# Cross-attention block in f32: the first context rows in two halves around the scale weights, block 0 projected in seven half-size products, and the way in in another order

## The chip, the cores and the metric

The kernel runs on one core of one Trainium2 chip. The metric is the device time of one execution in microseconds (us); the text names a version's time by the median of its runs. The profile is of one execution.

## The reference

An adaptive layer norm in front of a cross attention with 16 heads, and a residual. All arrays are f32: x is (16, 1024, 512), the context (16, 64, 512), the condition (16, 512), the weights 512 x 512 or 512 x 1024.

```python
def _ada_ln(x, c, W_ss, b_ss):
    h = (x - mean(x)) / sqrt(var(x) + 1e-5)
    scale, bias = split(silu(c) @ W_ss + b_ss, 2)
    return (1.0 + scale)[:, None, :] * h + bias[:, None, :]

xq  = _ada_ln(x,   cond, Wss_q,  bss_q)
xkv = _ada_ln(ctx, cond, Wss_kv, bss_kv)
q = (xq @ Wq + bq).reshape(B, 1024, 16, 32)
k, v = split((xkv @ Wkv + bkv).reshape(B, 64, 2, 16, 32), axis=2)
attn = softmax(einsum(q, k) / sqrt(32))
out = einsum(attn, v).reshape(B, 1024, 512)
return x + (out @ Wp + bp)
```

## The kernel before

The 16 x 1024 query rows are cut into 32 *blocks* of 512 rows (two to a batch entry). The 16 x 64 context rows make two *groups*, A (batch entries 0 to 7) and B (8 to 15), of 512 rows each, so that a group's rows, features, keys and values have the shapes of a block.

Every 512 x 512 x 512 multiplication, but for some projections, is done in seven *products* of half-size blocks instead of eight (Strassen's scheme in Winograd's form): each is four matmuls of 128x256 (eight records in the trace). It needs sums and differences of half weights (`column_sums`, `weight_sums`, each in four steps) and of half features (`feature_sums`, `row_sums`), which GpSimd makes, and for group A's features VectorE. The products accumulate in two PSUM banks; partial results are evicted (`context_out`, `query_out`, `query_added`, `added`) and for some the first bank is copied into the second as a seed (`query_seed`). The seven are called here product 1 to 7 of keys, values, queries (of a block) or of the projection.

A block passes these steps. `load_x` brings its rows (pool `xpool` with two slots for all rows: A, 0, B, 1, 2, ... take them in turn, and a load waits until the last reader of the block two before is done). `q_stats` takes mean and variance of each of four row tiles on VectorE; `q_scale` makes the reciprocal deviation (ScalarE Ln and Exp, then four small operations, on GpSimd, for A on VectorE); `hidden` normalises on ScalarE. `turn` transposes within 32x32 squares on VectorE, and `move` sends the squares to their places in 16 DMAs (half of them, for block 1, from GpSimd's queue). `scale_features` applies scale and shift on ScalarE. Block 0 and the groups are instead transposed on TensorE (`turned_products`, `turned_features`) and scaled on their way out of PSUM (`turned_scaled`, `modulated`). Then come the seven query products; `score_products` twice, for two halves of the keys, into two PSUM tiles each, which `maximum` (VectorE) and `copied` (ScalarE) read one after the other; `maxima` spreads the row maxima; `subtract` (GpSimd), `weights` (Exp, ScalarE), `total` (GpSimd), `row_total`, `inverse_rows` (VectorE, then small DMAs through DRAM), `mix` (TensorE, weights times values), `spread_rows` and `divided` (VectorE), and the projection: `row_sums`, `biased`, seven times `product` and `added`, which also adds the residual and stores.

Block 0 is projected otherwise: `project_seed` writes the bias into a bank and `project_seeded` runs four matmuls of 128x512 into it, for each of its four row tiles, followed by `projected`.

The values of a group are evicted into a stage and sent by `value_move` in 16 DMAs to their places.

Nothing is reordered by a scheduler: under `tc.manual_schedule()` each engine, and SP's DMA queue, executes its instructions in the order in which the program emits them, and waits where data, buffers or PSUM tiles are not free. The emission order of the way in, from the first load to the start of the loop over blocks 3 to 29, is a list written out by hand at the end of the function, interleaving all of the above. From block 3 on a loop emits a fixed order; TensorE's first step there is the score products of block 3 (160.10 us in the profile).

At the start SP issues the condition, the four row tiles of group A, the first half of the context's scale and shift weights (`wss_kv`), a quarter of the key and value weights, and so on; TensorE runs 36 warm-up transposes and then `scale_shift_rows`, which turns the condition and these weights into scale and shift rows.

Of the kernel before, what the change touches and what calls it, by code (L numbers as in the profile page):

```python
# [15 lines left out]
P = 128  # L16
# [4 lines left out]
def cross_attention_block(  # L21
# [84 lines left out]
    def load_x(i):  # L106

        t = xpool.tile([P, NT, H], F32, tag="x", name=f"x_{i}")
        if i in GROUPS:
            b = GROUPS[i] * PER  # L110
            rows = context[b : b + PER].rearrange("b k h -> (b k) h")
            src = rows.rearrange("(t p) h -> p t h", p=P)
        else:
            src = rows_of(x, i)
        if i == "A":
            for k in range(NT):
                nc.sync.dma_start(t[:, k, :], src[:, k, :])
        else:
            nc.sync.dma_start(t, src)
        x_tiles[i] = t  # L120

# [175 lines left out]
    def rstd_of(mv, n, apart):  # L297

        rstd = small.tile([P, 2, n], F32, tag="rstdq", name="rstdq")
        work = small.tile([P, 4, n], F32, tag="workq", name="workq")  # L300
# [29 lines left out]
    def q_scale(i):  # L330
        apart = i != "A"
        q_rstd[i] = rstd_of(q_mv.pop(i), NT, apart)
# [6 lines left out]
    def hidden(i, ts):  # L339

        for t in ts:
            row, rstd = x_tiles[i][:, t, :], q_rstd[i]
            if i == "A" and t % 2 == 0:
                nc.vector.tensor_scalar(
                    row, row, rstd[:, 0, t : t + 1], rstd[:, 1, t : t + 1], ALU.mult, ALU.add
                )
            else:
                normalise(row, row, rstd, t)
# [43 lines left out]
    def turned_features(i, t):  # L392
# [10 lines left out]
        if t == NT - 1:  # L403
            x_tiles.pop(i)
# [151 lines left out]
    def query_product(i, n):  # L556
        seven(i, "q", n, (0, 1))
# [306 lines left out]
    def project_seed(i, t):  # L864
        pp_tiles[i, t] = bank(f"pp_{i}_{t}", 2 + t % 2)
        nc.scalar.copy(pp_tiles[i, t], b_p_sb)

    def project_seeded(i, t):
        pp = pp_tiles[i, t]
        for c in range(NC):  # L870
            nc.tensor.matmul(  # L871
                pp,
                lhsT=ot_tiles[i][:, c, t * P : (t + 1) * P],
                rhs=w_p_sb[:, c, :],
                start=False,
                stop=(c == NC - 1),
                skip_group_check=True,
            )

# [13 lines left out]
    def weight_sums():  # L893

        tt = nc.gpsimd.tensor_tensor
        WT = wt[0] = wpool.tile([P, 4, HC, HO], F32, tag="WT", name="WT")
        tt(WT[:, 0], half_weights(0, 1), half_weights(1, 1), ALU.add)
        tt(WT[:, 1], WT[:, 0], half_weights(0, 0), ALU.subtract)
        tt(WT[:, 2], half_weights(0, 0), half_weights(0, 1), ALU.subtract)
        tt(WT[:, 3], half_weights(1, 0), WT[:, 1], ALU.subtract)  # L900

# [100 lines left out]
    turned_features("A", 0)  # L1002
    hidden("A", (1,))
    column_sums("k", w_k_sb, w_k_sums, (2,))
    column_sums("v", w_v_sb, wv_sums, (0,))
    scale_shift_taken("kv", 0)
    scale_shift("kv", 2 * NC, 0)
    hidden("A", (3,))
    turned_features("A", 1)
    column_sums("v", w_v_sb, wv_sums, (2,))  # L1010
    modulated("A", 0, 0, nc.scalar)
    modulated("A", 0, 0, nc.vector)
    turned_features("A", 2)
    turned_features("A", 3)
# [8 lines left out]
    modulated("A", 1, 0, nc.scalar)  # L1023
    modulated("A", 1, 1, nc.scalar)
    modulated("A", 1, 1, nc.vector)
    context_out("A", "k", 1)
    context_product("A", "k", 2)
    feature_sums("A", nc.vector, (0,))
    context_product("A", "v", 2)
    context_out("A", "k", 2)  # L1030
    context_product("A", "k", 7)
    column_sums("v", w_v_sb, wv_sums, (1,))
    context_out("A", "v", 1)
    column_sums("k", w_k_sb, w_k_sums, (1,))
    context_out("A", "v", 2)
    feature_sums("A", nc.vector, (1,))
    feature_sums("A", nc.vector, (2,))
    load_x("B")
    context_product("A", "v", 7)
    context_out("A", "k", 7)  # L1040
    q_stats(0, (0,))
    q_stats(0, (1,))
    context_out("A", "v", 7)
    q_stats(0, (2,))
    feature_sums("A", nc.vector, (3,))
    context_product("A", "v", 6)
    scale_shift_rows("q", 0)
    context_product("A", "k", 6)
    q_stats(0, (3,))
    load_query_weights()  # L1050
    scale_shift_rows("q", 1)
    context_out("A", "v", 6)
    context_product("A", "v", 4)
    scale_shift_taken("q", 0, 2)
    load_projection_bias()
    q_scale(0)
    scale_shift("q", 0, 0, 2)
    q_stats("B", (0,))
    context_product("A", "v", 5)
    q_stats("B", (3,))  # L1060
    column_sums("v", w_v_sb, wv_sums, (3,))
    q_stats("B", (2,))
    hidden(0, (0,))
    hidden(0, (1,))
# [548 lines left out]
```

## Time and profile before

| what | value |
|---|---|
| time, 3 runs | median 1029.23 us (1028.48 to 1030.68) |
| the profiled execution | 1029.09 us, span from the first to the last instruction 1027.3 us |
| mean granted TensorE clock | 0.998 |
| busy: TensorE (PE) | 1008.1 us, 98% |
| busy: VectorE (DVE), GpSimd (POOL), ScalarE (ACT) | 860.8, 805.9, 639.7 us |
| DMA | 149.82 MB, mean 146 GB/s |

How to read the rows: a row of the timeline has start and duration in us, engine, line of the kernel, operation, output <- inputs, the shape, how many instructions are merged, and in brackets the engine's idle time before it with what released it. A row of the waits has who waited for whom, and the total, the number and the longest of these waits. A row of the chain of waits has start, duration and what the chain was made of at that time. A row of the windows has the stretch, its length, the busy time of PE, PEld (weight loads), DVE, ACT and POOL, then the granted clock, the DMA share and GB/s. A row of the groups has line, engine, operation, shapes, count, busy time, the mean in ns, and the idle time before.

### The profile page before, as it was taken

How to read it: one execution, taken by the hardware profiler on the slowest of the kernel's cores; microseconds unless marked ns; L12 is line 12 of the kernel's file. 1: busy time of each engine (PE TensorE's matmuls, PEld its weight loads, DVE VectorE, ACT ScalarE, POOL GpSimd, SP SyncE). 2: the span in 40 equal slices, each digit the busy share in tenths (PEclk: the TensorE clock that was granted, in tenths of full speed). 3: DMA queues.
4: the chain of work that ended last, by engine and by line, in shares of the span. 5: the costliest groups of instructions: out<-in, count | busy, mean ns of one | idle time of the engine just before them, and what ended most of it. 6: DMA issues, size and time to landing. Idle time of an engine off the chain costs nothing.

```text
span 1027.3 us, 21213 instructions
## 1 busy us (share of the span) xinstructions
PE 1008.1 (98%) x8077; PEld 763.3 (74%) x8077; DVE 860.8 (84%) x1174; ACT 639.7 (62%) x1025; POOL 805.9 (78%) x518
## 2 busy tenths in 40 slices
PE   7989999999999999999999999999999999999998
PEld 6768657777777777877777778777777777777756
DVE  6757988888988888889888888888888888876795
ACT  3577667666766666666666667666675666665530
POOL 4547798789888888898888888988888888987861
PEclk9999999999999999999999999999999999999999
DMA  9555645444554444445544544545534444335122
GB/s 314 174 133 142 179 134 145 156 158 154 161 166 130 127 148 138 145 154 163 165 126 131 163 124 152 155 156 165 162 100 149 131 159 152 115 123 166 45 85 85
DMA packets 112197, 149.82 MB, mean 146 GB/s; under 512 B 34104, under 2 KB 45392, under 8 KB 112096
## 3 DMA queue, kind: packets, MB, share of 16 engines
q1 hardware_dynamic: 111712, 147.94, 46.8%
q8 instruction: 64, 1.05, 0.5%
q0 software_dynamic: 384, 0.54, 0.3%
q14 instruction: 37, 0.30, 0.1%
HBM read 79.21 MB, written 34.60 MB: 111 GB/s over the span
## 4 chain that ended last, share of the span: by engine, by line
PE 88%; DMA 3%; DVE 3%; ACT 2%; SPq 1%; issue 1%; POOL 1%; DVEq 0%; ACTq 0%; POOLq 0%
PE pq L539 36%; PE pp L955 34%; PE ps L658 6%; PE po L826 6%; PE pp L871 1%; PE pv_B L539 1%; DMA x<-in_x_dram 1%; PE pv_A L539 1%; DMA xt<-ht 1%; PE pk_A L539 1%; DMA wss_kv<-in_L_xcond_Wss_kv_dram 1%; SPq L387 1%; DVE m L675 1%; ACT s L723 1%; ACT xk_B L421 0%
## 5 line engine op out<-in xcount | busy, mean ns | idle before, releaser
L717 POOL TENSOR_TENSOR s<-s,mb 128x2048 f32<-128x2048 f32 x64 | 290.3, 4561 | 125.7 <-DVE mb L704 125.7
L684 ACT COPY s<-ps 128x1024 f32<-128x1024 f32 x128 | 129.6, 1013 | 105.3 <-DVE m L675 63.7
L675 DVE TRANSPOSE_TENSOR_REDUCE m<-ps 128x32 f32<-128x1024 f32 x128 | 151.0, 1215 | 32.1 <-PE ps L658 32.1
L955 PE MATMUL pp<-w_p_sb,ot 128*128 128x256 f32 x720 | 165.5, 379 | 0.5 <-DVE r L979 0.4
L979 DVE TENSOR_TENSOR r<-pp,r 128x512 f32<-128x512 f32 x203 | 132.0, 671 | 33.6 <-PE pp L955 29.4
L578 ACT ACTIVATE qt<-pq,bias_t 128x256 f32<-128x256 f32 x256 | 106.0, 465 | 80.4 <-PE pq L539 80.1
L955 PEld LDWEIGHTS pp<-w_p_sb,ot 128*128 128x128 f32 x720 | 136.6, 190 | 20.3 <-issue 1.3
L723 ACT ACTIVATE s<-s 128x2048 f32<-128x2048 f32 x64 | 122.4, 1913 | 43.2 <-POOL s L717 43.1
L757 POOL TENSOR_TENSOR sum<-s,s 128x2048 f32<-128x2048 f32 x31 | 140.7, 4538 | 7.8 <-ACT s L723 7.8
L955 PEld LDWEIGHTS pp<-WT,s 128*128 128x128 f32 x480 | 86.5, 189 | 57.0 <-issue 31.0
L539 PE MATMUL pq<-xt,w_q_sb 128*128 128x256 f32 x512 | 122.5, 382 | 4.5 <-ACT xt L447 4.5
L539 PE MATMUL pq<-xt_sums,w_q_sums 128*128 128x256 f32 x512 | 123.0, 385 | 0.0
L539 PEld LDWEIGHTS pq<-xt_sums,w_q_sums 128*128 128x128 f32 x512 | 95.0, 190 | 35.2 <-issue 23.4
L539 PE MATMUL pq<-xt,w_q_sums 128*128 128x256 f32 x512 | 120.9, 379 | 0.0
L955 PE MATMUL pp<-WT,s 128*128 128x256 f32 x480 | 119.3, 391 | 0.2 <-POOL s L934 0.2
L955 PE MATMUL pp<-WT,ot 128*128 128x256 f32 x480 | 113.7, 380 | 0.6 <-POOL ot L931 0.6
L539 PEld LDWEIGHTS pq<-xt,w_q_sb 128*128 128x128 f32 x512 | 97.3, 191 | 21.3 <-ACT xt L447 5.7
L539 PEld LDWEIGHTS pq<-xt,w_q_sums 128*128 128x128 f32 x512 | 97.3, 190 | 13.6 <-DVE ht L365 0.2
L955 PEld LDWEIGHTS pp<-WT,ot 128*128 128x128 f32 x480 | 91.0, 190 | 14.4 <-issue 1.1
L447 ACT ACTIVATE xt<-xt,ss_q 128x512 f32<-128x512 f32 x124 | 94.4, 810 | 10.1 <-DMA V_A<-stage_A 5.3
L335 ACT ACTIVATE x<-x,rstdq 128x512 f32<-128x512 f32 x128 | 97.8, 810 | 2.1 <-POOL rstdq L312 2.1
L498 POOL TENSOR_TENSOR xt_sums<-xt 128x512 f32<-128x512 f32 x64 | 81.5, 1273 | 17.0 <-ACT xt L447 9.5
(176 smaller groups left out, 1506.3 us busy)
## 6 DMA issues: line engine op xcount, KB each, us to landing
x<-in_x_dram SPq DMA_DIRECT2D x32, 1024.0 KB, 6.2
r<-in_x_dram SPq DMA_DIRECT2D x32, 1024.0 KB, 5.4
xt<-ht SPq DMA_DIRECT2D x488, 64.0 KB, 2.0
out_dram<-r SPq DMA_DIRECT2D x58, 512.0 KB, 3.7
out_dram<-r SPq DMA_DIRECT2D x11, 256.0 KB, 2.2
wss_kv<-in_L_xcond_Wss_kv_dram SPq DMA_DIRECT2D x4, 512.0 KB, 8.6
wss_q<-in_L_xcond_Wss_q_dram SPq DMA_DIRECT2D x4, 512.0 KB, 11.0
vr<-ltd SPq DMA_DIRECT2D x128, 8.0 KB, 1.7
```

The lines of the kernel that those rows point to most:

```text
L335: nc.scalar.activation(dst, src, AF.Identity, bias=rstd[:, 1, j : j + 1], scale=rstd[:, 0, j : j + 1])
L447: nc.scalar.activation(xt[:, :, c, :], xt[:, :, c, :], AF.Identity, scale=ss["q"][:, c, b : b + 1], bias=ss["q"][:, NC + c, b : b + 1],)
L498: eng.tensor_tensor(dst, a, b, ALU.subtract)
L539: nc.tensor.matmul(out_, lhsT=lhsT, rhs=rhs, start=new and m == 0 and c == 0, stop=c == HC - 1, skip_group_check=True,)
L578: nc.scalar.activation(dst, src, AF.Identity, bias=bq_t[:, o : o + 1])
L675: nc.vector.tensor_reduce(m_tiles[i][:, z, 2 * e : 2 * e + 2, :], s_banks[i, z][e].rearrange("p r (j a) -> p r j a", a=32), AX.X, ALU.max, ...
L684: nc.scalar.copy(s_tiles[i, z][:, 2 * e : 2 * e + 2, :], s_banks[i, z][e])
L717: eng.tensor_tensor(s_tiles[i, z], s_tiles[i, z], mb_tiles[i], ALU.subtract)
L723: nc.scalar.activation(p, p, AF.Exp, scale=SCALE)
L757: nc.gpsimd.tensor_tensor(t, s_tiles[i, 0], s_tiles[i, 1], ALU.add)
L955: nc.tensor.matmul(acc[k][:, t * HO : (t + 1) * HO], lhsT=rows[:, c, t * P : (t + 1) * P], rhs=cols[:, c, :], start=n == 2 and t == 0 and ...
L979: nc.vector.tensor_add(r, a, r)
```

## The change

Three things change.

1. The four row tiles of group A are loaded in two pairs: tiles 0 and 1 ahead of the first scale weights, tiles 2 and 3 behind these and the first key weights. Their statistics, Ln, Exp and the four small VectorE operations are done for each pair apart (`first_scale(h)` in place of `q_scale("A")`).
2. Block 0 is projected like the others: `biased`, `row_sums`, seven `product`, `added`. `project_seed` and `project_seeded` are gone. `weight_sums` takes a step's number, so that its four sums can be emitted apart.
3. The list of the way in is emitted in another order, up to the loop. On SP's queue the projection bias goes from behind the query weights to behind the load of block 3, half of group A's value moves go ahead of that load, and the move of block 3 goes ahead of the transfer of block 0's row totals. The loop and the end are as before.

The helpers:

```diff
-        if i == "A":
-            for k in range(NT):
-                nc.sync.dma_start(t[:, k, :], src[:, k, :])
-        else:
-            nc.sync.dma_start(t, src)
+        nc.sync.dma_start(t, context_rows(i) if i in GROUPS else rows_of(x, i))
         x_tiles[i] = t
...
+    def load_first(k):
+
+        if k == 0:
+            x_tiles["A"] = xpool.tile([P, NT, H], F32, tag="x", name="x_A")
+        nc.sync.dma_start(x_tiles["A"][:, k, :], context_rows("A")[:, k, :])
...
-    load_x("A")
+    load_first(0)
+    load_first(1)
     load_scale_shift("kv", w_ss_kv, 0)
     load_context_weights(0, 0)
+    load_first(2)
+    load_first(3)
     load_scale_shift("kv", w_ss_kv, 1)
...
     def q_scale(i):
-        apart = i != "A"
-        q_rstd[i] = rstd_of(q_mv.pop(i), NT, apart)
+        q_rstd[i] = rstd_of(q_mv.pop(i), NT, True)
+
+    def first_scale(h):
+        q_rstd["A", h] = rstd_of(q_mv["A"][:, 2 * h : 2 * h + 2, :], 2, False)
...
-    def weight_sums():
+    def weight_sums(k):
```

The order, at the places that the prediction speaks of (each list is whole between its first and last line; "..." where lines are left out):

```diff
 start of group A: the old order (-), the new (+)
-    q_stats("A", (0,))
-    q_stats("A", (1,))
-    q_stats("A", (2,))
-    q_stats("A", (3,))
-    column_sums("k", w_k_sb, w_k_sums, (0,))
-    biases()
-    q_scale("A")
-    hidden("A", (0,))
-    hidden("A", (2,))
-    scale_shift_rows("kv", 0)
...
-    context_product("A", "k", 1)
-    scale_shift_rows("kv", 1)
-    modulated("A", 0, 1, nc.vector)
-    scale_shift_taken("kv", 1)
-    scale_shift("kv", 2 * NC, 1)
-    modulated("A", 0, 1, nc.scalar)
-    modulated("A", 1, 0, nc.vector)
-    context_product("A", "v", 1)
+    column_sums("k", w_k_sb, w_k_sums, (2,))
+    q_stats("A", (0,))
+    q_stats("A", (1,))
+    scale_shift_rows("kv", 0)
+    first_scale(0)
+    hidden("A", (0,))
+    biases()
+    scale_shift_taken("kv", 0)
+    scale_shift("kv", 2 * NC, 0)
+    turned_features("A", 0)
...
+    modulated("A", 0, 0, nc.scalar)
+    modulated("A", 0, 0, nc.vector)
+    q_stats("A", (3,))
+    load_x("B")
+    q_stats("A", (2,))
+    first_scale(1)
+    hidden("A", (2,))
+    hidden("A", (3,))
+    context_product("A", "k", 1)
+    scale_shift_rows("kv", 1)
+    scale_shift_taken("kv", 1)
+    turned_features("A", 2)
+    context_out("A", "k", 1)
+    column_sums("v", w_v_sb, wv_sums, (0,))
+    scale_shift("kv", 2 * NC, 1)
...
+    modulated("A", 1, 1, nc.scalar)
+    context_product("A", "k", 2)
+    context_product("A", "v", 1)
```

```diff
 after, around block 1's rows: statistics, normalising, turning, moving
+    q_stats(1, (3,))
+    context_product("A", "v", 4)
+    turned_features("B", 1)
+    value_move("A", 0)
+    column_sums("q", w_q_sb, w_q_sums, (1,))
+    q_stats(1, (1,))
...
+    turned_features("B", 0)
+    modulated("B", 0, 0, nc.vector)
+    turned_features("B", 3)
+    load_x(3)
+    turned_features("B", 2)
...
+    query_seed(0)
+    modulated("B", 1, 0, nc.scalar)
+    hidden(1, (0,))
+    query_product(0, 6)
+    query_product(0, 2)
+    context_out("B", "k", 1)
+    hidden(1, (1,))
+    turn(1, (0,))
...
+    turn(1, (3,))
+    query_out(0, 2)
...
+    move(1, two=True)
```

```diff
 after, score products of block 1 and the row total of block 0
+    score_products(1, 0)
+    context_out("B", "v", 6)
+    maximum(1, 0, 1)
+    row_total(0)
+    maximum(1, 0, 0)
+    context_product("B", "v", 5)
...
+    query_product(2, 1)
+    copied(1, 0, 1)
+    copied(1, 0, 0)
...
+    score_products(1, 1)
```

```diff
 before, block 0's projection (for t = 0 to 3, interleaved)
-    project_seed(0, t)
-    project_seeded(0, t)
-    projected(0, t)
...
-    weight_sums()
 after
+    row_sums(0, 0)
...
+    product(0, 2)
...
+    product(0, 1)
...
+    weight_sums(0)
+    weight_sums(2)
+    weight_sums(1)
...
+    row_sums(0, 1)
...
+    product(0, 7)
```

More of the change, by code (lines that the diff above doesn't have):

```diff
@@ L1077, in cross_attention_block @@
     q_scale("B")
[L1078 removed]
+    turned_scaled(3)
+    column_sums("q", w_q_sb, w_q_sums, (2,))
+    turned_scaled(1)
+    turned_scaled(0)
+    hidden("B", (0,))
+    load_x(2)
     q_stats(1, (0,))
[L1080 to L1081 removed]
+    hidden("B", (3,))
+    hidden("B", (1,))
+    feature_sums(0, nc.gpsimd, (0,))
+    q_stats(1, (2,))
     context_product("A", "k", 3)
[L1083 to L1084 removed]
@@ L1197, in cross_attention_block @@
-    feature_sums(1, nc.gpsimd, (2,))
-    query_out(1, 2)
-    maximum(0, 1, 0)
-    maximum(0, 1, 1)
-    maxima(0)
+    hidden(3, (0,))
+    maximum(0, 1, 1)
+    query_product(1, 2)
+    context_product("B", "k", 3)
+    maximum(0, 1, 0)
+    query_out(1, 2)
+    feature_sums(1, nc.gpsimd, (2,))
+    query_product(1, 7)
+    context_out("B", "k", 3)
+    feature_sums(1, nc.gpsimd, (3,))
+    maxima(0)
+    hidden(3, (3,))
+    q_stats(4, (0,))
+    copied(0, 1, 1)
+    move(2)
+    load_projection()
@@ L1366, in cross_attention_block @@
-    weights(2, 0)
-    subtract(2, zs=(1,))
-    row_sums(1, 0)
+    load_x(6)
+    biased(0, 3)
+    copied(2, 0, 0)
+    feature_sums(3, nc.gpsimd, (1,))
+    product(0, 7)
+    maximum(2, 0, 1)
+    maximum(2, 0, 0)
+    copied(2, 0, 1)
+    move(4)
+    added(0, 7)
+    query_out(3, 2)
+    score_products(2, 1)
+    product(0, 6)
+    maximum(2, 1, 0)
+    copied(2, 1, 0)
+    feature_sums(3, nc.gpsimd, (2,))
+    product(0, 4)
+    hidden(5, (2,))
+    maximum(2, 1, 1)
+    weight_sums(3)
@@ new lines, in cross_attention_block @@
+    added(0, 6)
+    product(0, 5)
+    feature_sums(3, nc.gpsimd, (3,))
+    q_stats(6, (0,))
+    copied(2, 1, 1)
+    maxima(2)
+    hidden(5, (3,))
+    inverse_rows(1)
+    hidden(5, (1,))
+    mix(1)
+    query_product(3, 7)
+    hidden(5, (0,))
+    subtract(2, zs=(0,))
+    turn(5, (0,))
+    q_stats(6, (2,))
+    turn(5, (1,))
+    added(0, 5)
+    added(0, 4)
+    product(0, 3)
+    query_out(3, 7)
+    scale_features(4, (2,))
+    subtract(2, zs=(1,))
+    query_product(3, 6)
+    spread_rows(1)
```

550 lines of the change are left out of this document (227 added, 323 removed).

## The prediction

> **What bounds the kernel now.** I read the page first, then for whom TensorE waited, then the chain of waits and the windows around the longest wait.
>
> ```profile
> span 1027.3 us, 21213 instructions
> ...
> PE 1008.1 (98%) x8077; PEld 763.3 (74%) x8077; DVE 860.8 (84%) x1174; ACT 639.7 (62%) x1025; POOL 805.9 (78%) x518
> ```
>
> TensorE's waits in the first 260 us (in total, times, longest):
>
> ```profile
> PE pq L539 <- ACT xt L447: 4.5, 1, 4.5
> PE pc L218 <- DMA early<-in_cond_dram: 2.6, 1, 2.6
> PE pq L539 <- ACT qt L578: 1.4, 1, 1.4
> PE pxk_B L400 <- DVE xk_B L419: 1.3, 1, 1.3
> PE pxk_A L400 <- DVE xk_A L419: 1.1, 1, 1.1
> PE ps_kv L256 <- DMA wss_kv<-in_L_xcond_Wss_kv_dram: 1.0, 1, 1.0
> PE po L826 <- ACT s L684: 0.4, 1, 0.4
> ```
>
> TensorE is busy for all but 19 us, and 12 of these lie here, nearly all in the way in. The loop from block 3 on is full, and the change leaves its order alone. So the question is when TensorE comes to the loop, at 160.1 us now, and with what behind it. From the chain of waits (start, duration, eight matmul records to a product):
>
> ```profile
> 76.79 3.03 PE pq L539 x8
> 79.83 2.37 PE pk_B L539 x8
> ```
>
> ```profile
> 122.28 3.43 PE pp L871 x8
> 125.71 1.73 PE pq L539 x8
> ```
>
> and from the windows (TensorE's granted clock is the third number from the end):
>
> ```profile
> 40.00:60.00 20.00, 18.66 (x95) 16.38 (x94) 13.51 (x37) 17.39 (x45) 15.35 (x20) 1.00 0.29 103
> ```
>
> ```profile
> 78.00:80.00 2.00, 2.00 (x6) 1.60 (x5) 1.97 (x4) 1.94 (x6) 1.27 (x1) 0.50 0.43 105
> ```
>
> A product takes 1.73 us. The two behind the 4.5 us wait took 3.03 and 2.37, 1.9 more than usual, at a clock of 0.50. I count 1.75 of it, so the longest wait costs 6.2 us in all. After the 1.3 us wait, which falls in 40 to 60 us, the clock stayed at 1.00.
>
> **The change, part by part.** I take the new order of each engine's instructions, give each the duration it has in these rows, and follow who waits for whom.
>
> *Block 0.* Four projections of 3.43 us, 13.72 in all, become seven products of 1.73, 12.11: 1.6 us less for TensorE. The price is four row sums on GpSimd, taken up below; the four weight sums are there before and after.
>
> *The first context rows.* From TensorE's timeline, twice, with the chain between:
>
> ```profile
> 8.88 0.41 PE L256 MATMUL ps_kv<-wss_kv,early 128*32 128x128 f32 x4
> 10.30 1.07 PE L256 MATMUL ps_kv<-wss_kv,early 128*32 128x128 f32 x28 [1.00 <-DMA wss_kv<-in_L_xcond_Wss_kv_dram]
> ```
>
> ```profile
> 14.70 1.73 PE pk_A L539 x8
> ```
>
> ```profile
> 38.47 5.44 DMA x<-in_x_dram
> 43.94 0.70 DVE bs L294
> 44.67 0.18 DVE mvq L295
> 44.85 0.57 DVE K_A L605
> 45.42 0.60 DVE stage_A L619
> 46.02 1.02 DVE xk_B L419 x4
> ```
>
> ```profile
> 48.45 1.89 PE L539 MATMUL pq<-xt,w_q_sb 128*128 128x256 f32 x8
> ```
>
> Two of the four row pieces now go behind the scale weights. At most 1.4 us is to be had (8.88 to 10.30); I take 1.25, so the scale rows start at 9.05. The bias transpose and its two vector copies now lie behind them (about 0.5), while eight transposes (about 1.1) are no longer ahead of the first product, which waits for a modulation instead: key product 1 of group A starts near 13.5, 1.2 earlier than 14.70. But the second half of the rows now has its statistics, Ln, Exp and four small vector instructions of its own behind the first modulations. They end near 16.5, and the modulated rows are ready only at 18.9. Before, value product 1 filled that place; now key product 2 stands first and waits 1.25, and with it both value products behind it and the evictions on ScalarE and VectorE that follow them. The early start is spent.
>
> The transposes of block 0 then end near 37.4 (before, 38.4), with value product 4 still to come. They release the slot that block 1 loads into: rows there at 37.4 + 5.5 = 42.9. The order now puts all four statistics of block 1 (0.8 each, 0.70 and the rest of the step) and a value eviction (0.6) ahead of the first modulation of group B (1.02): 47.8. TensorE is through with what it has at 46.0, waits 1.85, and still has four transposes (0.6) and key product 4 (1.73). The first query product of block 0 starts at 50.2 against 48.45: 1.75 lost, a little from each place.
>
> *The longest wait.* From the timelines of VectorE, SP's queue, GpSimd and ScalarE:
>
> ```profile
> 60.68 1.30 DVE L365 STREAM_TRANSPOSE ht<-x 128x512 f32<-128x512 f32 x2
> ```
>
> ```profile
> 62.47 6.50 SPq L387 DMA_DIRECT2D xt<-ht  x8
> 69.02 11.45 SPq L631 DMA_DIRECT2D V_A<-stage_A  x16
> ```
>
> ```profile
> 63.50 4.08 POOL L387 DMA_DIRECT2D xt<-ht  x8
> ```
>
> ```profile
> 74.52 2.22 ACT L447 ACTIVATE xt<-xt,ss_q 128x512 f32<-128x512 f32 x3 [5.30 <-DMA V_A<-stage_A]
> ```
>
> Block 1 is turned by 62.0; 12.5 us later its moved features are scaled, because the 1 MB load of block 3 goes ahead of the moves and the value moves mix with them. In the new order ScalarE normalises block 1 right behind two accumulator copies instead of among query evictions, so block 1 is turned at 57.8, although TensorE is later. Ahead of the moves on SP's queue now stand that load and the 256 KB projection bias (between nothing and a quarter of 5.44; I take 0.75); half the value moves are already out. I keep 12.5 + 0.75: features there at 71.0 (bounds 69, if the missing half of the value moves counts, and 73, if they mix worse). ScalarE reaches them at 71.8, behind a key eviction and a score copy, and has the first two scaled at 73.3. TensorE wants them behind thirteen products and a score pair, as before, which took 23.9 (48.45 to 76.79 less the wait of 4.5): 50.2 + 23.9 = 74.1. So this wait goes, with about a microsecond to spare, and its clock loss too: the product starts 2.7 earlier and loses 1.75 less, 4.45 together. Late next is the second score pair of block 0, whose banks are free only after the transposes of block 2 and one more maximum (75.0, wanted at 75.8).
>
> *Score pairs of block 1.* VectorE and ScalarE:
>
> ```profile
> 104.16 2.31 DVE L762 TRANSPOSE_TENSOR_REDUCE lt<-sum 128x64 f32<-128x2048 f32 x1 [0.60 <-POOL sum L757]
> ```
>
> ```profile
> 106.97 2.31 DVE L675 TRANSPOSE_TENSOR_REDUCE m<-ps 128x32 f32<-128x1024 f32 x2
> ```
>
> ```profile
> 108.19 1.01 ACT L684 COPY s<-ps 128x1024 f32<-128x1024 f32 x1 [0.62 <-DVE m L675]
> ```
>
> The row total of block 0 (2.31) now stands between the two maxima of the first pair (1.16 each), and a copy (1.01) follows each maximum: from the end of the first pair it takes 4.6 + 1.0 us until both banks are free, while TensorE has two products and half a pair to do. It waits 1.6 (0 if the total comes out of the way, 2.2 if the half pair covers nothing). Behind it wait value product 3 of group B, a query product and the attention product of block 0, whose own 0.4 us goes. On SP's queue the move of block 3 now stands ahead of the transfer of block 0's row totals (about 2 us later out); the division they serve ends near 116.6, when product 2 of block 0 is due, so I cost it at nothing, and a microsecond more of it would be seen one to one.
>
> *GpSimd.*
>
> ```profile
> 115.66 9.06 POOL L717 TENSOR_TENSOR s<-s,mb 128x2048 f32<-128x2048 f32 x2 [0.30 <-DVE mb L704]
> ```
>
> ```profile
> 160.10 1.33 PE L658 MATMUL ps<-qt,K_A 32*32 32x512 f32 x32
> 161.37 1.99 PE L955 MATMUL pp<-WT,s 128*128 128x256 f32 x8
> ```
>
> Product 6 of block 1 (161.37) reads a row sum of GpSimd's, which from the subtraction of block 1 on is nearly always at work: 45.7 us to there. The four row sums of block 0, 1.28 each, add 5.1, of which about 1.7 falls into old idle. By the walk above the maxima of block 1 are spread at 108.6, so product 6 starts at 108.6 + 45.7 + 5.1 - 1.7 = 157.7. TensorE, 4.45 + 0.4 - 1.6 (score pairs) + 1.6 (block 0) = 4.85 early, would want it at 156.5. It waits 1.2, there or for the division of block 1 just ahead, and 3.7 is left.
>
> *The sum* stands against the profiled execution's own time (1027.3 span, 1029.09 in all, 0.14 below the median of 1029.23). In the loop, the 1.4 us wait hangs on a feature move of block 5 that goes out late; it now goes out about a microsecond earlier against TensorE, and I take half, 0.7. 3.7 + 0.7 = 4.4: **1024.7 us**.
>
> The new waits of 1.85 and 1.6 lose nothing by the clock here, like the 1.3 us one, the nearest row. In proportion to the longest wait (1.75 on 4.5) they would lose 1.4, and the sum be 1026.1. [...]
>
> **The rivals.** *(a) The new waits aren't there.* Without the 1.25, 1.85, 1.6 and 1.2, 5.9 in all, of which I let four through since features and GpSimd then become late: 1020.7. For it: each rests on two engines' orders within a microsecond or two. Against: each follows from an order that is written down. *(b) The gain is half eaten:* features of block 1 land at 75 instead of 71, because the moves of two queues mix with eight value moves; a 3 us wait comes back without the clock loss, 1027.7. *(c) Slower: GpSimd becomes the bound.*
>
> ```profile
> 24.46 1.71 POOL L472 TENSOR_TENSOR w_k_sums<-w_k_sums,w_k_sb 128x512 f32<-128x512 f32 x1
> ```
>
> ```profile
> L934 POOL TENSOR_TENSOR s<-ot,s 128x512 f32<-128x512 f32 x21 | 26.8, 1275 | 0.0
> ```
>
> Beside VectorE's sums in the way in, one weight sum took 1.71. If all 15 small sums between 108 and 158 us do so, that adds 6.6: product 6 starts at 164.3 after a wait of 7.8, and the clock falls again (1.75): 1029.1 + 2.9 + 1.75 - 0.7 = 1033.0. It decides from a sum ready later than 161.1, where the gain is gone. Against it: in the loop (300 to 900 us) 21 such sums took 1.275 beside a full VectorE. *(d) The halves don't bring the scale weights forward,* since transfers run side by side: 1.25 less, 1025.9, within my range.
>
> **How the numbers follow.** My forecast with (d) 0.55, (a) 0.17, (b) 0.13, (c) 0.15. About 0.2% (2 us) is what a measurement of this kernel tells from no change: faster 0.72, from the forecast and (a); same 0.12, most of (b); slower 0.16, (c) and a rest of (b). The range goes from 1020.0, just past (a), to 1030.5, past (b); (c) lies outside.
>
> **What would show it.** Right: scale rows at about 9; waits for a modulation near 18 and 47; no wait of over 2 us at the first query product of block 1, near 74, and no clock under 1.00 there; a wait at the second score pair of block 1, near 101; scores of block 3 near 156, and a row sum of GpSimd's that ends last at product 6 of block 1. Wrong: the first query product of block 0 later than 52, or the wait near 74 still over 3 us with a clock of 0.50, or product 6 of block 1 later than 161.

## The result and the profile after

The changed kernel takes 1026.64 us (median of 11 runs, 1024.15 to 1028.87), the kernel before, run beside it, 1029.64 (11 runs, 1028.48 to 1031.05). The ratio is 0.9971, with a 95% interval from 0.9961 to 0.9982: 3.0 us faster, where 4.4 had been forecast. The profiled execution of the changed kernel took 1026.66 us.

The page, and TensorE's waits in the first 260 us (in total, times, longest; pc, the wait for the very first load, is as before):

```profile
span 1024.9 us, 21278 instructions
...
PE 1008.3 (98%) x8101; PEld 768.9 (75%) x8101; DVE 863.4 (84%) x1181; ACT 639.2 (62%) x1025; POOL 810.2 (79%) x522
```

```profile
PE pxk_B L407 <- DVE xk_B L424: 2.3, 1, 2.3
PE pk_A L544 <- ACT xk_A L426: 1.6, 2, 0.8
PE ps L663 <- ACT s L689: 1.1, 1, 1.1
PE ps_kv L260 <- DMA wss_kv<-in_L_xcond_Wss_kv_dram: 0.9, 1, 0.9
PE pk_A L544 <- DVE xk_sums_A L503: 0.8, 1, 0.8
PE ps_kv L282 <- DVE early L273: 0.7, 1, 0.7
```

The 4.5 us wait is gone, and in its place stand several of about one to two microseconds. Yet TensorE is as busy as before, although 1.6 us of its work was taken out. The warm-up transposes took 0.86 us longer in this execution (6.34 against 5.48), and a stretch at half clock stands here as it did before, at another place. TensorE's timeline (start, duration):

```profile
3.17 6.34 PE L986 MATMUL warm<-ident 128*128 128x128 f32 x36
...
10.72 1.07 PE L260 MATMUL ps_kv<-wss_kv,early 128*32 128x128 f32 x28 [0.86 <-DMA wss_kv<-in_L_xcond_Wss_kv_dram]
...
14.63 2.15 PE L544 MATMUL pk_A<-xk_A,w_k_sb 128*128 128x256 f32 x8 [0.79 <-ACT xk_A L426]
...
20.22 2.15 PE L544 MATMUL pk_A<-xk_A,w_k_sb 128*128 128x256 f32 x8 [0.79 <-ACT xk_A L426]
...
26.62 1.97 PE L544 MATMUL pk_A<-xk_sums_A,w_k_sums 128*128 128x256 f32 x8 [0.79 <-DVE xk_sums_A L503]
...
50.38 0.63 PE L407 MATMUL pxk_B<-ident,x_B 128*128 128x128 f32 x4 [2.29 <-DVE xk_B L424]
...
52.58 1.89 PE L544 MATMUL pq<-xt,w_q_sb 128*128 128x256 f32 x8
...
76.29 1.89 PE L544 MATMUL pq<-xt,w_q_sb 128*128 128x256 f32 x8
...
104.30 2.17 PE L663 MATMUL ps<-qt,K_A 32*32 32x512 f32 x32 [1.13 <-ACT s L689]
106.40 3.52 PE L544 MATMUL pv_B<-wv_sums,xk_B 128*128 128x256 f32 x8
...
159.56 1.14 PE L663 MATMUL ps<-qt,K_A 32*32 32x512 f32 x32
160.64 1.99 PE L950 MATMUL pp<-WT,s 128*128 128x256 f32 x8
```

The scale rows start at 10.72 (10.30 before), the first query product of block 0 at 52.58 (48.45 before), 4.1 late. At the first query product of block 1, 76.29, there is no wait: the 4.1 us and another half are won back here, and the product takes its usual time. Then the second score pair of block 1 waits, and the value product behind it takes 3.5 us. The windows around it (granted clock third from the end) show why:

```profile
106.00:108.00 2.00, 2.00 (x18) 1.31 (x5) 1.97 (x3) 0.64 (x2) 1.41 (x2) 0.68 0.41 101
108.00:110.00 2.00, 2.00 (x6) 1.64 (x5) 1.97 (x2) 2.00 (x3) 0.00 (x0) 0.50 0.11 18
110.00:112.00 2.00, 2.00 (x24) 1.46 (x39) 1.36 (x3) 1.25 (x2) 1.32 (x1) 0.97 0.22 44
```

The clock falls there to 0.50 for 3.4 us (0.32, 0.50 and 0.03 are missing in three stretches of 2 us, 1.7 us of full clock), after a wait of 1.13 and a second one of about 1.03 inside the pair, which the merged row hides: its 32 matmuls take 2.17 instead of 1.14. So the scores of block 3 start at 159.56, only 0.54 earlier than the 160.10 of before.

### The profile page after: what moved, and what is told of

It is laid out like the page before. It is cut to its first block, busy times and chain, and to the rows that moved or that the text cites. A ratio compares the mean times of both kernels' runs of the same rounds, so it can differ in the third digit from the quotient of the medians.

```text
span 1024.9 us, 21278 instructions
## 1 busy us (share of the span) xinstructions
PE 1008.3 (98%) x8101; PEld 768.9 (75%) x8101; DVE 863.4 (84%) x1181; ACT 639.2 (62%) x1025; POOL 810.2 (79%) x522
## 4 chain that ended last, share of the span: by engine, by line
PE 92%; DVE 3%; DMA 2%; SPq 2%; POOL 1%; ACT 1%; issue 0%; DVEq 0%; POOLq 0%; ACTq 0%
PE pq L544 38%; PE pp L950 36%; PE ps L663 7%; PE po L831 7%; PE pk_B L544 1%; PE pv_B L544 1%; DMA wss_q<-in_L_xcond_Wss_q_dram 1%; SPq L144 1%; DVE m L680 1%; PE pk_A L544 1%; DMA x<-in_x_dram 1%; PE pv_A L544 1%; SPq L167 1%; POOL s L722 0%; DVE lt L767 0%
## 5 line engine op out<-in xcount | busy, mean ns | idle before, releaser
L950 PE MATMUL pp<-w_p_sb,ot 128*128 128x256 f32 x744 | 171.0, 379 | 0.5 <-DVE r L974 0.4
L974 DVE TENSOR_TENSOR r<-pp,r 128x512 f32<-128x512 f32 x210 | 136.6, 671 | 32.9 <-PE pp L950 28.0
L950 PEld LDWEIGHTS pp<-w_p_sb,ot 128*128 128x128 f32 x744 | 141.2, 190 | 20.9 <-issue 1.3
L950 PEld LDWEIGHTS pp<-WT,s 128*128 128x128 f32 x496 | 89.4, 189 | 58.2 <-issue 26.8
L950 PE MATMUL pp<-WT,s 128*128 128x256 f32 x496 | 123.2, 391 | 0.2 <-POOL s L929 0.2
L950 PE MATMUL pp<-WT,ot 128*128 128x256 f32 x496 | 117.6, 380 | 0.7 <-POOL ot L926 0.6
L950 PEld LDWEIGHTS pp<-WT,ot 128*128 128x128 f32 x496 | 93.8, 190 | 15.3 <-issue 1.6
```

The lines of the kernel that those rows point to most:

```text
L950: nc.tensor.matmul(acc[k][:, t * HO : (t + 1) * HO], lhsT=rows[:, c, t * P : (t + 1) * P], rhs=cols[:, c, :], start=n == 2 and t == 0 and ...
L974: nc.vector.tensor_add(r, a, r)
```

## The experiments

Every ratio is against the kernel before, run on the same chip beside it. The kernel before took 1029.64, 1029.29 (beside e1, e2, e3, e7), 1029.12 and 1029.60 us (beside e9, e10, c1, c2), so that half a microsecond between medians of different rows can come from that alone. Since the clock turned out to matter, the last column counts the executions whose mean granted clock was at least 0.999: one fall like the one above takes 1.7 us of 1025, and leaves 0.998.

| kernel | median us (runs) | ratio, 95% interval | clock 0.999 or more |
|---|---|---|---|
| before (beside e4, e5, e6, e8) | 1029.12 (21) | | 0 of 21 |
| after | 1026.64 (11) | 0.9971 [0.9961, 0.9982] | 2 of 11 |
| e1 total behind the maxima | 1027.45 (12) | 0.9977 [0.9967, 0.9986] | 2 of 12 |
| e2 and own buffer | 1024.80 (6) | 0.9964 [0.9949, 0.9978] | 4 of 6 |
| e3 four projections | 1033.61 (6) | 1.0054 [1.0038, 1.0070] | 0 of 6 |
| e7 = e2 + e3 | 1033.28 (6) | 1.0048 [1.0032, 1.0065] | 0 of 6 |
| e4 modulation first | 1024.32 (5) | 0.9960 [0.9946, 0.9973] | 3 of 5 |
| e5 before, wait filled | 1027.13 (11) | 0.9980 [0.9971, 0.9989] | 11 of 11 |
| e6 old start | 1025.39 (5) | 0.9962 [0.9950, 0.9975] | 2 of 5 |
| e8 four projections, moves ahead | 1030.32 (11) | 1.0015 [1.0006, 1.0025] | 4 of 11 |
| e9 block 1 late | 1033.10 (12) | 1.0032 [1.0020, 1.0043] | 0 of 12 |
| e10 before, seven products | 1044.62 (4) | 1.0156 [1.0138, 1.0173] | 0 of 4 |
| c1 = e6 + e4 | 1023.54 (5) | 0.9944 [0.9929, 0.9958] | 1 of 5 |
| c2 = c1 + score pair | 1023.81 (5) | 0.9945 [0.9932, 0.9958] | 4 of 5 |

**e1: is it the order of the maxima?**

```diff
     maximum(1, 0, 1)
-    row_total(0)
     maximum(1, 0, 0)
+    row_total(0)
```

> The changed kernel with the row total of block 0 behind both maxima of the first score pair of block 1, instead of between them. Theory P, the prediction's own step (TensorE waits at the second score pair because the row total stands between the two maxima): the maxima end at 102.1 instead of 104.3, the copies follow, the wait there (1.13 and, between the two halves of the pair, about 1.05) and the slow clock behind it (about 1.8) go; what is left of that is decided further on, 1022.7 to 1026. Theory B (the copies themselves wait for the row total, because the sum that it reads lies in the buffer that they write): the row total ends 1.2 later, at 104.4, the copies begin there, the pair starts near 105.5, the wait grows to about 2.3 and everything behind it is 1.2 late: 1027.8.

ScalarE's and TensorE's timelines of e1:

```profile
103.93 1.93 ACT L689 COPY s<-ps 128x1024 f32<-128x1024 f32 x2 [4.33 <-DVE lt L767]
```

```profile
104.99 2.51 PE L663 MATMUL ps<-qt,K_A 32*32 32x512 f32 x32 [2.26 <-ACT s L689]
```

The copies stand idle for 4.33 us and start when the row total (`lt`) is done; the wait is 2.26, as theory B had it (about 2.3). The prediction's step put it down to the order of the maxima, and that falls. The copies write the buffer `big2` in which `total(0)` put its sum, so they can't start before the row total has read it. In time, e1 and the changed kernel can't be told apart (their intervals overlap).

**e2: another buffer for that sum.** As e1, and

```diff
-big, f"big{(i + 1) % 2 * 2}"
+big, "big3" if i == 0 else f"big{(i + 1) % 2 * 2}"
```

> As the run before, and the sum of block 0 lies in another buffer (the one that held the key weights), so that the copies need not wait for the row total. Theories P and B: no wait and no slow clock at the second score pair of block 1 (it starts near 103.2), TensorE 3.5 to 4 us earlier from there. If TensorE sets the time, all of it arrives: about 1022.7. Theory G (GpSimd sets the arrival in the loop: from the subtraction of block 1 on it works without a break, and that starts with the maxima of block 1, which VectorE ends hardly earlier): the subtraction starts at 110.4 instead of 110.7, TensorE waits some 3 us for GpSimd or what hangs on it before product 6 of block 1, the scores of block 3 are at most 0.7 earlier, 1026.0, or 1.7 later than that if the clock falls there.

TensorE's timeline of e2:

```profile
49.41 0.63 PE L407 MATMUL pxk_B<-ident,x_B 128*128 128x128 f32 x4 [2.33 <-DVE xk_B L424]
49.88 3.24 PE L544 MATMUL pk_A<-xk_sums_A,w_k_sb 128*128 128x256 f32 x8
...
103.81 1.18 PE L663 MATMUL ps<-qt,K_A 32*32 32x512 f32 x32
106.18 1.99 PE L544 MATMUL pv_B<-wv_sums,xk_B 128*128 128x256 f32 x8 [1.19 <-DVE stage_B L629]
...
120.66 1.97 PE L950 MATMUL pp<-w_p_sb,ot 128*128 128x256 f32 x8 [0.91 <-PE pq L544]
```

The pair no longer waits, but the value product behind it does (1.19, its bank is evicted behind the row total), and so does product 2 of block 0 (0.91): its division hangs on the row total, which now ends later. In this execution the scores of block 3 start at 159.56, exactly as in the changed kernel. This execution's clock fell at another place, behind the 2.33 us wait at 49.4, where the key product takes 3.24. Four of six executions showed no fall at all. The wait for GpSimd that theory G names isn't there. What e2 gains is then better explained by fewer falls than by less waiting; with six runs of e2 this is argued, not shown.

**e3, e7, e8: block 0 by four projections again.** e3 undoes the second part of the change alone; e7 does so on top of e2.

```diff
-    biased(0, 2); row_sums(0, 0); product(0, 2); ... added(0, 3)
+    project_seed(0, 0); project_seeded(0, 0); ... projected(0, 3)
```

> The changed kernel with block 0 projected by the four old projections; everything else in the new order. It takes 5.1 us of row sums from GpSimd and adds 1.6 to TensorE. If TensorE sets the time: scores of block 3 1.6 later, 1028.2. If GpSimd set it, so that TensorE's 1.6 us are not seen: no change or up to 1 us faster, 1025.6 to 1026.6.

> Both: the sum of block 0 in its own buffer with the row total behind the maxima, and block 0 by the four old projections. Theory G: GpSimd is 5.1 us freer, so the 3.5 to 4 us of the score pair now arrive, less the 1.6 of the projections: 1024.4, about 1.6 faster than the buffer alone. If TensorE sets the time by itself: 1.6 slower than the buffer alone, 1024.3 against 1022.7. So the sign between this run and the one with the buffer alone tells the two apart.

Both cost some 7 us, which no theory had, and e7 tells nothing beyond e3, since the same wait stands in both. GpSimd's waits in e3 (110 to 165 us):

```profile
POOL WT L905 <- DMA V_B<-stage_B: 9.9, 1, 9.9
```

`WT`, the weight sums, reuses the buffer of `stage_B`, and the moves that read it had gone out on SP's queue behind a store of block 0, which waits for its projection. e8 mends that:

```diff
     weights(1, 0)
+    value_move("B", 1)
     project_seed(0, 1)
...
     row_total(1)
-    value_move("B", 1)
```

> The changed kernel with block 0 projected by the four old projections again, and now with the second half of group B's value moves ahead of the stores of block 0 on SP's queue, since in the first try they went out behind a store, and GpSimd's weight sums, which reuse the buffer that the moves read, waited 9.9 us for them. The prediction's term (seven products are worth 1.6 us): scores of block 3 1.6 later than in the changed kernel, 1028.2. If GpSimd's row sums had set the time: 1025.6 to 1026.6. If the first try's 7 us weren't due to that wait: 1033.

```profile
136.40 1.47 PE L663 MATMUL ps<-qt,K_A 32*32 32x512 f32 x32 [1.10 <-ACT s L689]
...
153.30 1.99 PE L544 MATMUL pq<-xt,w_q_sums 128*128 128x256 f32 x8 [0.70 <-ACT qt L583]
156.67 3.69 PE L966 MATMUL pp<-w_p_sb,ot 128*128 128x256 f32 x16 [1.38 <-DVE ot L811]
```

(TensorE's timeline of e8; the profiled execution is 2.1 us slower than the median.) Undoing now costs 3.7 us in the median (1030.32 against 1026.64). In the profile there are the 1.6 of the work and new waits of 1.1, 0.7 and 1.4. That GpSimd has 5.1 us less to do brings nothing that shows, and none of these waits is for it. The term of 1.6 alone isn't isolated.

**e10: the seven products alone, in the kernel before.**

```diff
-    project_seed(0, 0); project_seeded(0, 0); ... projected(0, 3); weight_sums()
+    biased(0, 2); product(0, 1); ... weight_sums(); row_sums(0, 1); ... added(0, 3)
```

> The kernel before with nothing of the change but block 0's seven products (with the two value moves of group B ahead of them, so that the weight sums find their buffer free). The prediction's term: 1.6 us less work on TensorE; if nothing else waits, 1027.6. If the division of block 1, the evictions or GpSimd's nine small sums (four row sums now lie ahead of the subtraction of block 2) come late instead: 1029.3 or slower.

TensorE's waits (110 to 165 us) of e10, and GpSimd's timeline:

```profile
PE pp L955 <- POOL WT L899: 7.4, 1, 7.4
PE ps L658 <- ACT s L684: 3.1, 1, 3.1
```

```profile
137.07 1.26 POOL L897 TENSOR_TENSOR WT<-w_p_sb 128x512 f32<-128x512 f32 x1 [4.24 <-DMA V_B<-stage_B]
```

15 us slower. The weight sums, needed one block earlier than before, meet the same buffer as in e3: GpSimd stands 4.24 us for the value moves that read `stage_B`, although these were put ahead, and the third sum is ready only at 140.9, where product 7 of block 0 wants it at 133.6. The seven products save TensorE's time only in an order made for them; this run says nothing on the 1.6 either.

**e4: the modulation ahead of the statistics.**

```diff
-    q_stats(1, (3,)) ... q_stats(1, (1,))
     ...
     modulated("B", 0, 0, nc.vector)
+    q_stats(1, (3,))
+    q_stats(1, (1,))
```

> The changed kernel with two of the four statistics of block 1 behind the first modulation of group B on VectorE instead of ahead of it. Theory C (the clock falls in windows of 3.4 us, at a place that differs from one execution to the next, after any wait of 1 to 2.3 us; each such fall costs 1.7): the wait for the modulation falls from 2.3 to about 0.7, the first query product of block 0 starts near 51.0, and more executions show a clock of 1.000; 1.6 us and part of a fall, 1024.5. If what TensorE gains here is given back further on (to the features of block 1, the score pair or GpSimd): 1026.6.

TensorE's timeline of e4:

```profile
47.73 0.63 PE L407 MATMUL pxk_B<-ident,x_B 128*128 128x128 f32 x4 [0.85 <-ACT xk_B L426]
...
49.93 1.89 PE L544 MATMUL pq<-xt,w_q_sb 128*128 128x256 f32 x8
...
101.65 2.17 PE L663 MATMUL ps<-qt,K_A 32*32 32x512 f32 x32 [1.13 <-ACT s L689]
103.75 1.99 PE L544 MATMUL pv_B<-wv_sums,xk_B 128*128 128x256 f32 x8
...
154.80 1.14 PE L663 MATMUL ps<-qt,K_A 32*32 32x512 f32 x32
```

1024.32, 2.3 less than the changed kernel (1.8 when each is taken against the kernel before beside it; the intervals overlap). The wait is 0.85 instead of 2.29. The rows of the score pair say more: it is the same pair with the same wait of 1.13 as in the changed kernel's profile, to the digit, and here the product behind it takes 1.99, not 3.52. Of the seven profiles with this wait the clock fell behind it in four (changed kernel, e6, e9, c1) and not in three (e3, e4, e8). Whether it falls there differs between executions. This execution had no fall at all and is the fastest of e4 (1022.04).

**e5: the wait stays, the idleness goes.** In the kernel before:

```diff
+    fill = bank("fill", 0)
+    for _ in range(44):
+        nc.tensor.transpose(fill[:, :P], ident, ident)
     query_product(1, 1)
```

> The kernel before with 44 transposes of the identity, which nothing reads, put on TensorE ahead of the first query product of block 1, so that it works through 4 of the 4.5 us that it waits there. Nothing else is changed, and the features come no sooner. The prediction's step (the slow clock behind the wait comes from TensorE's idleness and costs 1.75): the product starts at 76.8 as before and takes 1.73 instead of 3.03, the granted clock stays at 1.00 from 74 to 82, 1.7 us faster, 1027.5. If the clock fell for another reason, or the gain is given back before the loop: 1029.3.

```profile
73.00 4.97 PE L1178 MATMUL fill<-ident 128*128 128x128 f32 x44
78.07 1.96 PE L539 MATMUL pq<-xt,w_q_sb 128*128 128x256 f32 x8
...
159.66 1.33 PE L658 MATMUL ps<-qt,K_A 32*32 32x512 f32 x32
```

(TensorE's timeline of e5.) 1027.13 against 1029.12: work that nobody reads makes the kernel 2.0 us faster, with 1.7 expected. All 11 executions had a clock of 0.999 or more, and they lie within 1.7 us of each other; none of 21 executions of the kernel before reached 0.999. The profile shows the clock's share: from the first query product of block 1 to the scores of block 3 it takes 81.59 us here and 83.31 before (76.79 to 160.10), in the same order of instructions, 1.72 less. The product itself starts later than the 76.8 expected, since this execution was 0.8 late already at block 0 (49.27 against 48.45) and the transposes took 4.97 us instead of 4. So the 2.0 of the medians is not that share alone: the fillers cost up to half a microsecond, and 13 of the 21 executions before had a mean clock of 0.997 or less, which is more than one fall's worth.

**e6: the start undone.** Loads, statistics and order of before up to key product 7 of group A, from there the new order.

```diff
     load_first(0)
     load_first(1)
+    load_first(2)
+    load_first(3)
     load_scale_shift("kv", w_ss_kv, 0)
     load_context_weights(0, 0)
-    load_first(2)
-    load_first(3)
```

> The changed kernel with the start undone: the four row tiles of group A loaded ahead of the scale weights, one set of statistics, and the order of before up to key product 7 of group A; from there the new order. The prediction's step (the start in halves wins 1.25 and spends it on a wait for the modulation; it measured worse than that): key product 1 at 14.7, no wait for a modulation near 18 and none for the feature sums near 26, the transposes of block 0 end about 1.5 to 2 earlier, at 38, and the first query product of block 0 starts near 51 instead of 52.6: about 1.6 faster, 1025.0, if it arrives in the loop, 1026.6 if not. If the halves did bring something that the trace doesn't show at once (an earlier load of block 1): slower, 1027.5 or more.

TensorE's timeline of e6:

```profile
10.18 1.18 PE L260 MATMUL ps_kv<-wss_kv,early 128*32 128x128 f32 x32
...
47.70 0.63 PE L407 MATMUL pxk_B<-ident,x_B 128*128 128x128 f32 x4 [2.04 <-DVE xk_B L424]
...
49.90 1.89 PE L544 MATMUL pq<-xt,w_q_sb 128*128 128x256 f32 x8
...
156.98 1.14 PE L663 MATMUL ps<-qt,K_A 32*32 32x512 f32 x32
```

In these two profiles the scale rows start at 10.18, not later than with the halves (10.72). The first query product of block 0 is 2.7 earlier than in the changed kernel, and all of it arrives at the scores of block 3 (2.6 earlier, in an execution with one fall of the clock, like the changed kernel's). Part of the 2.7 is chance, for the other profiles with the new start and the same modulation order come there between 50.05 and 53.05. Two stretches separate the parts. The scale rows end between 9.88 and 11.79 in the eight profiles with the new start and between 11.13 and 12.34 in the six with the old one, 0.6 earlier on average. From there to the first query product of block 0 it takes 38.5 us in e6 and 40.2 to 41.0 in the four with the new start that wait for the same modulation and have no fall on the way (changed kernel, e1, e3, e7), about 2 more. So the new start loses more by its order than the halves bring. The median is 1.25 less (0.7 when each is taken against the kernel before beside it), and the intervals overlap.

**e9: block 1 normalised and turned late.**

```diff
-    hidden(1, (1,)); turn(1, (0,)); ... hidden(1, (3,)); ... turn(1, (3,)); query_out(0, 2)
+    turn(1, (0,)); ... query_out(0, 2); hidden(1, (1,)); turn(1, (1,)) ... query_out(0, 6); hidden(1, (3,)); turn(1, (3,))
     move(1, two=True)
```

> The changed kernel with block 1 normalised and turned late again: one row tile at a time between the key and query evictions, as before the change. The prediction's step (the longest wait goes because block 1 is turned 4 us earlier, and is worth 4.5 us and a clock fall of 1.75): block 1 is turned near 65 instead of 60.4, its features land near 78, the wait for them at its first query product comes back with 3 to 5 us and the clock falls behind it in every execution, 1030 to 1032. If what lies on the DMA queues ahead of the moves decides instead: features at 75, wait under 1, 1026.6 to 1027.5.

GpSimd's and TensorE's timelines of e9:

```profile
66.38 4.03 POOL L394 DMA_DIRECT2D xt<-ht  x8 [7.44 <-DVE ht L372]
70.41 1.29 POOL L503 TENSOR_TENSOR xk_B<-xk_B 128x512 f32<-128x512 f32 x1
```

```profile
73.97 3.78 PE L544 MATMUL pk_B<-xk_sums_B,w_k_sums 128*128 128x256 f32 x8 [3.59 <-POOL xk_sums_B L503]
```

6.5 us slower than the changed kernel, 1.1 past the expected range (part of it by the clock, a mean of 0.993 in the profiled execution), but by a third way: GpSimd stands 7.4 us before its eight moves, which wait for the turned rows, and then issues them for 4.0, and the feature sums of group B behind them on its queue are late. TensorE waits for those at 74, and no longer for the features. So it is shown that block 1 must be turned early; how long TensorE would have waited for the features themselves stays open.

**c1 and c2: what the experiments point to.** c1 is e6 and e4 together; c2 adds to it, at the first score pair of block 1:

```diff
+    (the sum of block 0 in big3, as in e2)
-    maximum(1, 0, 1); row_total(0); maximum(1, 0, 0)
+    maximum(1, 0, 0); row_total(0); maximum(1, 0, 1)
-    inverse_rows(0)
+    context_out("B", "v", 5); inverse_rows(0)
-    copied(1, 0, 1); copied(1, 0, 0)
+    copied(1, 0, 0); copied(1, 0, 1)
```

> The changed kernel with the old start and with the first modulation of group B ahead of two statistics of block 1, the two edits that each were faster alone (1025.39 and 1024.32 against 1026.6). If they add up: the wait for the modulation about 0.7 and the first query product of block 0 near 48.5, 1023.0. If the features of block 1 or GpSimd now are late, so that the second edit's gain is given back: 1024.3 to 1025.4.

> As the run before, and at the first score pair of block 1: the sum of block 0 in its own buffer, the row total between the maxima with the first half's maximum and copy first, and value product 5's eviction ahead of the reciprocal. Theory B (copies wait for the row total through the shared buffer): the second pair starts without a wait, at most 0.6 between its halves, 1.5 us less and hardly a fall of the clock left: 1021.5, with a clock of 1.000 in most executions. If the division of block 0 or GpSimd eats it: as the run before, 1023.0.

c1 takes 1023.54, 3.1 us less than the changed kernel and 6.1 less than the kernel before beside it; its interval ends below where the changed kernel's begins. c2 brings nothing more. TensorE's timeline of c2:

```profile
101.59 1.09 PE L663 MATMUL ps<-qt,K_A 32*32 32x512 f32 x16 [1.06 <-ACT s L689]
...
116.59 1.97 PE L950 MATMUL pp<-w_p_sb,ot 128*128 128x256 f32 x8 [0.87 <-PE pq L544]
```

The pair's second half still waits 1.06 instead of at most 0.6, and product 2 of block 0 waits 0.87 for a division that hangs on the later row total, as in e2. The fall of the clock is gone in four of five executions, yet the median is not lower. In the profiles c2 takes 60.20 us from the first score pair of block 1 (94.73) to the scores of block 3, and c1 61.01 (from 95.53), although c1 has a fall of 1.7 and the wait of 1.13 in it and c2 has neither: 2.0 of these 2.8 are given back behind the pair, 0.87 of it at the division. What is left doesn't show in the medians of five runs.

## Why the prediction was right in sign and short in size

**The account.** By the prediction's walk TensorE would reach the loop 4.85 us early, with 3.7 left behind a wait at product 6; in the profile it came 0.54 early. Of the 4.3 that is missing, about 2.4 was lost by the first query product of block 0 (52.58 for 50.2), 0.6 at the second score pair of block 1 (2.2 for 1.6) and 1.7 to the clock behind it; 0.2 was won on the walk between.

**Right: the longest wait.** It went, with its slow clock. The walk of 23.9 us from the first query product of block 0 to that of block 1 measured 23.71 (52.58 to 76.29). It was not TensorE's lateness that hid the wait: in e6 TensorE comes there 2.7 earlier (73.61) and doesn't wait either. The clock's share is shown by e5's profile: 1.72 against the 1.75 counted.

**Wrong: the start.** In this execution the 1.25 us for the halves did not come: the wait for the scale weights is still 0.86, and the rows start at 10.72, where 9.05 was forecast. That is partly chance. The time at which the weights are there and the length of the warm-up transposes (5.48 us in the profile before, 6.34 after, 6.86 in e8, 6.81 with the old start in e6) differ from one execution to the next; in five of the eight profiles with the new start there is no wait for the weights, and over all profiles about half of the 1.25 came (e6). So rival (d) is neither shown nor excluded. Further on, value product 2 ended at 25.8 instead of about 24.1 (two waits of 0.8 for a modulation, one forecast of 1.25), and a wait for the feature sums that I had not seen followed (0.79, at 26.62). These sums took 1.7 us on VectorE beside GpSimd's weight sums, and 0.69 alone:

```profile
24.75 1.72 DVE L503 TENSOR_TENSOR xk_sums_A<-xk_A 128x512 f32<-128x512 f32 x1
25.88 1.73 POOL L477 TENSOR_TENSOR wv_sums<-wv_sums,w_v_sb 128x512 f32<-128x512 f32 x1
26.51 1.64 DVE L503 TENSOR_TENSOR xk_A<-xk_A 128x512 f32<-128x512 f32 x1
28.18 0.69 DVE L503 TENSOR_TENSOR xk_sums_A<-xk_A 128x512 f32<-128x512 f32 x1
```

(VectorE's and GpSimd's timelines after; GpSimd's next row starts at 33.84.) I had that row from GpSimd's side, 1.71 against 1.27, and used it for rival (c) alone. With the wait at pxk_B (2.29 for 1.85) the first query product of block 0 came at 52.58 for 50.2, past the mark of 52 that I had named. e6 and e4 show that both losses, of the start and at pxk_B, were real and reach the loop.

**Wrong in its reason: the second score pair of block 1.** 1.6 forecast, about 2.2 measured (1.13 and 1.03). Not the order of the maxima but a shared buffer makes the copies wait (e1).

**Wrong: that waits like these lose nothing by the clock.** I took the 1.3 us row of before as proof. In the changed kernel waits of 1.13 and 1.03 were followed by 3.4 us at half clock; in e2 it was the 2.33 us wait. Only 2 of 11 executions went without any fall. This is the largest miss at one place: about 1.7 us in the profiled execution (value product 3, 3.31 from start to start instead of 1.73, and a little of the next). The prediction's other line, 1.4 in proportion to the length of the waits (1.34 by its own numbers; 1026.1), came close to the time, but for another reason: a fall costs 1.7 or nothing, and the executions differ. The falls measured here come to about 3.4 us at 0.50 (in three stretches of 2 us the clock was 0.90, 0.50 and 0.75 behind the 4.5 us wait of before, and 0.68, 0.50 and 0.97 in the changed kernel, 1.70 us of full clock missing both times; in e6 it was 0.55 and 0.59 in two, 1.72 missing), and behind the same waits they come in some executions and not in others; what decides that, no run here tests.

**Not seen: GpSimd as the next bound.** The 1.2 us at product 6 of block 1 weren't there, nor was rival (c): TensorE itself came late, GpSimd's row sums stayed at 1.3 us each, and e6's 2.6 us and e4's early arrival came through (product 6 of block 1 at 155.87 without a wait, where the walk had 157.7 as GpSimd's earliest). But it is close: in the profiles of the changed kernel, e2, e4, e6, c1 and c2 the row sum that product 6 reads ends only 0.4 to 0.5 us before the product starts.

**Not shown: 1.6 for block 0.** Undoing it costs more (e8), doing it alone costs far more (e10), each through new waits.

**A size that was chance: 0.7 in the loop.** From the scores of block 3 to the end of the span the profiled executions took 867.2 us before and 865.3 after. But the same loop took 865.4 in e5, which has the order of before, and 866.6 and 867.1 in e1 and e2, which have the new one. The 1.4 us wait of before is one that comes and goes with the execution: e5 has none, e1 and e2 have 1.1 and 1.2 us of waits for the same evictions. So of the 2.4 us between the two profiled spans, 0.54 came from the way in and 1.9 from the loop's scatter. The medians differ by 3.0. How that splits between arrival, falls of the clock and loop isn't settled by two profiles, and that 3.0 came as near to 4.4 as it did is in part luck.

## What to carry to other kernels

When a long wait is broken up into several short ones, price the clock for each: here a wait of one or two microseconds cost another 1.7 in some executions, and then the median moves with their share. Before putting a wait down to the order of instructions, ask which buffer the waiting instruction writes and who still reads that slot: here such a buffer tied steps together that have no data in common (the score copies of e1 waited 4.33 us behind a row total, the weight sums of e3 9.9 us behind value moves). And an early start is worth only what it brings at the first product that waited: here about 0.6 of the 1.25 us came on average, and the reordering around it cost about 2. Before reading the difference of two profiles, look at how far executions of the same order lie apart.

## What the runs showed of the hardware

- After waits of 1.13 + 1.03 us the granted clock fell in four profiled executions (changed kernel, to 0.50 for about 3.4 us, e6, e9, c1), and not after the same waits in three others (e3, e4, e8). The value product behind them took 3.52 us in the changed kernel, 3.33 in e6 and 3.30 in e9, and 1.99 in e4 and e8.
- After the 4.5 us wait of before no execution kept a mean clock of 0.999 (0 of 21), and with that wait filled all did (11 of 11).
- One such fall cost TensorE 1.7 us: 1.72 by the profiles of before and e5, 1.7 by the windows of the changed kernel.
- 36 warm-up transposes took 5.48 us in the profiled execution before, 6.34 after, and 6.45 to 6.86 in those of e5, e6, e8, e9, e10 and c2, with the same instructions.
- In the changed kernel's profile VectorE's feature sums of group A (128x512) took 1.72 and 1.64 us beside GpSimd's weight sums, and 0.69 alone; one of these weight sums took 1.73 there.
